# A two-layer attention and feed-forward kernel: exponentials of two chunks added before their sums are taken, and a written order for part of layer 0

## The chip, the cores and the metric

The kernel runs on one core of a Trainium2 chip. A core has five engines with a queue each: TensorE (PE in the profile, with its weight loads as PEld), VectorE (DVE), ScalarE (ACT), GpSimd (POOL) and SyncE (SP), which issues most of the transfers from memory. Each engine works through its queue in order; work of different engines runs side by side unless one waits for another. The metric is the device time of one execution in microseconds (us), the median over runs; smaller is better.

## What is computed

Eight batches of 112 tokens of 512 channels pass through two layers. Layer 0 is attention with one head over 375 memory rows per batch, then a feed-forward network (1408 hidden channels) with activations rounded to 8 bits and weights rounded to -1, 0 or 1. Layer 1 is attention with 16 heads of 32 channels over the same 375 rows, then a feed-forward network with integer weights. Cut to the part whose arithmetic changes:

```python
q, k, v = proj(hs, Wq, bq), proj(at, Wk, bk), proj(at, Wv, bv)   # 16 heads of 32
scores = clip(einsum('bhsd,bhtd->bhst', q, k) / sqrt(32), -50, 50)
scores = clip(where(attend, scores, -10000), -50, 50)
probs = softmax(scores, axis=-1)                 # over the 375 memory rows
ctx = einsum('bhst,bhtd->bhsd', probs, v)
...
x = x + layer0_attention(layernorm(x)); x = x + layer0_ffn(layernorm(x))
x = x + layer1_attention(layernorm(x)); x = x + layer1_ffn(layernorm(x))
```

The kernel takes no maximum in layer 1: it exponentiates the clipped scores, sums them over the keys (the denominator), multiplies them with the values (the numerator) and divides at the end.

## The kernel before, in words

**Layer 1 attention** (stage from 258 us to 417 us of the profile). A batch's 375 keys are three chunks of 125. The loop runs over batches b and chunks c; a step is written (b, c) here. In each step `scores(b, c)` makes, for four groups r of heads, a matmul of keys with queries into PSUM (L734), a clip on DVE (L739) into an SBUF tile `e` of 125 x 448, and an exponential in place on ACT (L740). `fill(1)` then puts one step of the key and value projection for later batches on PE (L176 for keys, evicted by ACT in L178; L183 for values, L185). `sums` of the step before puts on PE eight matmuls of `ones` with the four `e` (L754, the denominator `den`) and 32 of values with `e` (L759, the numerator `num`). `den` and `num` are evicted by ACT (L765, L766) after a batch's third chunk, and `divide` takes a reciprocal (L770) and a product (L772) on DVE one step later. `STEPS` says in which steps of a batch a `fill` is made: three per batch, but two in batches 4, 5 and 6. The tiles `e` have eight buffers, two steps' worth.

Around this run, two and three batches later, the output projection and its normalisation. `project_begin(i)` in step (i+2, 2) is a matmul L648 on PE, then on DVE L651, statistics, L659, and on GpSimd a reciprocal square root of seven short instructions (L97, L100, L101), L657, and a 128 x 512 addition L658. `project_end(i)` in step (i+3, 0) is on DVE L664, which needs L658, more statistics, and another such chain on GpSimd. `write4` is L678, `transpose4` is L685 on PE, L688 on ACT and L689 on DVE.

Integer weights of the last network are brought in meanwhile. `load_integers` issues a transfer of a piece of 128 x 512 integers on SP into one of three buffers `raw`; `convert_integers` makes a square on ACT (L721, with a read of its sum) and a conversion on GpSimd (L723), after which the buffer is free. `due` says how many pieces are converted in which step. In a step the order of the queues is: conversion, scores, fill, sums, then the rest. In (7, 2) a check `over` on GpSimd (L792) reads the sums of all squares, and a matmul of it (L795) stands on PE ahead of L648.

All five engines follow the written order in this stage.

**Layer 0** (up to 258 us). The attention loop over b makes `scores0(b)` (L365, a maximum L371 on DVE, an exponential L375 on ACT), `readout0(b-1)` (L394, L396 on DVE, and a transfer of the finished rows to `tokens` issued by GpSimd, L402), `transpose0(b+1)` of the normalised tokens written by `write0(b+1)` (L141 on DVE, then L358 on PE, L360 on ACT), a `fill` and `turn0(b)` (L387, L389). Between these, a string `BETWEEN` (three entries per batch) puts steps of two other works: a digit m is one step of rounding weight matrix m (`ternary`: four sums of magnitudes on ACT, L230; one step of a totals matmul L234 with L236, L237 and L240 on DVE; four steps of L244 on DVE and L245 on ACT), and a p is one step of `prepare(0, 2)`, which readies two tiles of 128 tokens for the feed-forward network in four steps: moments and reciprocal root on DVE; normalised values on DVE with squares (L263) on ACT and maxima (L264) on DVE; scales, a chain of short DVE instructions; rounding, L305 on ACT and L307 on DVE.

Layer 0's network runs over seven tiles i. `gate_up0(i)` makes six matmul groups on PE (L501), three activations on ACT (L505) and three products on DVE (L506), then a square (L263) on ACT, a maximum (L264) and a chain of short instructions that ends in the scale `fwd` (L274) on DVE, then the rounding L512 on ACT and L515 on GpSimd. `fill`, `turn_gate0` and `turn_down0` (L317, L319) and `down0` (L526) follow. All groups of L501, L176, L183, L394 and L526 share four PSUM tiles called `mm`: a group waits until the engine that empties a tile has done so. PE and SP follow the written order everywhere; DVE, ACT and GpSimd follow it in the attention loop of layer 0 and in layer 1's attention, and are ordered by a planner elsewhere, which may also put work written later among written work.

The functions below are `prepare`, `ternary`, the loop of layer 0, `gate_up0`, `load_integers`, `scores` and `sums`.

Of the kernel before, what the change touches and what calls it, by code (L numbers as in the profile page):

```python
# [35 lines left out]
P = 128  # L36
# [20 lines left out]
CLIP = 50.0 / SC1  # L57
WIDE = 4000.0 ** 2
# [4 lines left out]
def two_layers(ctx: ExitStack, tc: tile.TileContext, x, ctxT, ctxN, mask0, mask1, w1, w2, w3,  # L63
# [147 lines left out]
    with tc.tile_pool(name="w0", bufs=1, side="right") as w0p, \  # L211
# [9 lines left out]
        def ternary(m):  # L221

            rows = stat.tile([P, KC], F32, name="w_rows")
# [15 lines left out]
            scale = stat.tile([P, 1], F32, name="w_scale")  # L239
# [16 lines left out]
        def quantizers(srcs, n, name, squares):  # L256
# [3 lines left out]
            ss = stat.tile([P, m], F32, name=f"{name}_ss")  # L260
            mx = stat.tile([P, m], F32, name=f"{name}_mx")
# [7 lines left out]
            lim = stat.tile([P, m], F32, name=f"{name}_lim")  # L269
            nc.vector.tensor_mul(lim, mx, r)  # L270
            nc.vector.tensor_scalar_max(lim, lim, Q_EPS)
            fwd = stat.tile([P, m], F32, name=f"{name}_fwd")
# [3 lines left out]
            def back(mean, which):  # L276
                t = stat.tile([P, m], F32, name=f"{name}_back{which}")
                nc.vector.tensor_scalar(t, lim, mean, 1.0 / 127.0, ALU.mult, ALU.mult)
                return t
            yield fwd, back  # L280

        rooms = {}

# [26 lines left out]

        def transposed_h(q, n, name, pool):
# [14 lines left out]
        with tc.tile_pool(name="work0", bufs=2, side="right") as work0:  # L326
# [7 lines left out]
            def load_x(b0, b1):  # L334
                t = work0.tile([T, b1 - b0, D], F32, name=f"x0_{b0}", bufs=1)
                nc.sync.dma_start(out=t, in_=x[b0:b1].rearrange("b t d -> t b d"))
                x0.extend(t[:, b, :] for b in range(b1 - b0))
# [24 lines left out]
            def scores0(b):  # L362
# [7 lines left out]
                top = stat.tile([T, 1], F32, name="top")  # L370
# [3 lines left out]
                den = stat.tile([T, 1], F32, name="den")  # L374
# [59 lines left out]
            for i in range(4):  # L434
# [12 lines left out]
            BETWEEN = ["", "", "000", "0", "0", "1", "1", "0", "0", "0", "0", "1", "1", "1", "1",  # L447
                       "1", "1", "1p", "p", "2", "2p", "p", "2", "2"]
            preparing = prepare(0, 2)

            def between(b, n):
                for m in BETWEEN[3 * b + n]:
                    if m == "p":
                        next(preparing)
                    else:
                        steps_of(int(m), 1)

            with tc.manual_schedule(engines={ENGINES.PE, ENGINES.SP, ENGINES.DVE,
                                             ENGINES.Activation, ENGINES.Pool}):
                between(0, 2)  # L460
                for b in range(1, B):
                    if b < B - 1:
                        write0(b + 1)
                    scores0(b)
                    between(b, 0)
                    shares0(b)
                    if b > 1:
                        readout0(b - 1)
                    if b + 1 < B:
                        load_ctxN(b + 1)  # L470
                    if b + 2 < B:
                        cTs[b + 2] = load_ctxT(b + 2)
                    elif b + 2 == B:
                        cTs[2] = load_ctxT(2)
                    if b == 2 or b == 4:
                        load_raw(2, b // 2 - 1)
                    if b < B - 1:
                        transpose0(b + 1)
                    between(b, 1)
                    fill(1)  # L480
                    turn0(b)
                    between(b, 2)
                fill(1)
                turn_gate0(0)

                nc.scalar.activation(stat.tile([T, 1], F32, name="top"), s0[B - 1][1], AF.Silu)
                readout0(B - 1)


        with tc.tile_pool(name="work1", bufs=2, side="right") as work1:  # L490
            q3 = {}

            def gate_up0(i):
                qT = q1[i]
                gu = work1.tile([P, H], F32, name="gu")
                for n0, n in HBLK:
                    gate = ps_mm.tile([P, 512], F32, name="mm")
                    up = ps_mm.tile([P, 512], F32, name="mm")
                    for ps, w in ((gate, wqs[0]), (up, wqs[1])):
                        for kc in range(KC):  # L500
# [6 lines left out]
                                                   act[:, :n], ALU.mult, ALU.mult)  # L507
                q = work1.tile([P, H], BF16, name="q3")
                ranges = quantizers([gu], H, "q3", [q])
                next(ranges)  # L510
                fwd, back = next(ranges)
# [18 lines left out]
            for i in range(NT):  # L530
                if i == 2:
                    list(prepare(4, NT))
                gate_up0(i)
                if i == 0:
                    steps_of(2, 1)
                fill(1)
                if i == 0:
                    turn_gate0(1)
                    list(prepare(2, 4))
                fill(1)  # L540
                if i == 0:
                    steps_of(2, 1)
                elif i == 1:
                    steps_of(2, 2)
                if i:
                    turn_down0(i - 1)
                if 0 < i < NT - 1:
                    turn_gate0(i + 1)
                if i:
                    fill(1)  # L550

                if i == 1:
                    steps_of(2, 1)
                elif i == 2:
                    down0(0)
                if i > 1:
                    down0(i - 1)
# [71 lines left out]
    sd_s = load(tailp, sd.to_broadcast([P, D]), [P, D], "sd", nc.gpsimd)  # L629
# [7 lines left out]
    pieces = list(range(35))  # L637
# [54 lines left out]
    with tc.tile_pool(name="work2", bufs=1, side="right") as work2, \  # L692
# [6 lines left out]
        todo = [(w, which, half, c, min(D, HALVES[which][half + 1] - c))  # L699
                for which, w in enumerate((wg, wu, wd)) for half in range(2)  # L700
                for c in range(HALVES[which][half], HALVES[which][half + 1], D)]
        due = {(0, 1): 2, (0, 2): 2, (1, 0): 2, (1, 1): 2, (1, 2): 2, (2, 0): 2,
               (3, 1): 2, (3, 2): 2, (4, 0): 2, (5, 1): 2, (5, 2): 2, (6, 0): 2,
               (6, 1): 2, (6, 2): 2, (7, 0): 2, (7, 1): 2, (7, 2): 3}
# [296 lines left out]
```

## Time and profile before

| what | value |
|---|---|
| median of three runs | 538.13 us (537.45 to 540.0) |
| profiled execution, whole | 537.93 us |
| its span, first to last instruction | 536.1 us |
| mean granted TensorE clock | 0.995 |
| L754, denominator matmuls | 192, 23.8 us busy together |
| L658, addition on GpSimd, 128 x 512 | 7, median 1.279 us |
| L770, reciprocal on DVE | 8, 2.944 us each |
| L739 on DVE, four of a step | 2.45 us |
| L740 on ACT, four of a step | 2.35 us |
| L721 on ACT, and the read of its sum | 0.722 us and 0.190 us |
| L723 on GpSimd | median 0.617 us |
| `raw`, issue to landing | 2.5 to 25.2 us, median 2.9 |

A group's row names the line, the engine and the operation, what it writes and reads, how often, its busy time and the mean of one. Matmuls overlap: eight L754 take 0.96 us from the first start to the last end, and move the chain of waits by 0.89 us. A step's time on PE is best taken from that chain.

### The profile page before, as it was taken

The page shows a single profiled execution, that of the slowest core. Times are in us where ns is not written, and L with a number is a line of the kernel's source. Part 1 is how long each engine was busy: PE and PEld are TensorE (multiplying, and loading weights), DVE is VectorE, ACT ScalarE, POOL GpSimd, SP SyncE. Part 2 cuts the span into 40 slices and gives each one's busy share as a digit, 9 for nine tenths or more (in the row PEclk, how much of TensorE's full clock was granted, in tenths as well). Part 3 has the DMA queues.
Part 4 walks back from the last instruction along what each step waited for, and adds up shares of the span by engine and source line. Part 5 has one row for each costly group of instructions (what it writes and reads, how often), then busy time and mean ns, then how long its engine had stood idle before and what let it go on. Part 6 is the DMA issues. An engine that isn't in the chain of part 4 may idle for free.

```text
span 536.1 us, 8884 instructions
## 1 busy us (share of the span) xinstructions
PE 516.8 (96%) x3430; PEld 315.0 (59%) x3430; DVE 312.1 (58%) x769; ACT 247.2 (46%) x439; POOL 91.4 (17%) x197
## 2 busy tenths in 40 slices
PE   8998998989999999999999999999999999999995
PEld 6544554544455554545565555565654688889984
DVE  2552458769834755544546657988985764434432
ACT  1234754759644444402576545556766233203320
POOL 0000210101111101140121033523653540000000
PEclk9998999999999999999999999999999999999999
DMA  8994976300010120240123202102221000010001
GB/s 246 333 404 172 354 257 244 97 17 0 15 44 1 60 117 1 78 159 0 40 71 90 79 2 70 40 2 70 80 78 42 1 2 0 1 59 21 0 21 44
DMA packets 13312, 45.76 MB, mean 85 GB/s; under 512 B 1985, under 2 KB 2512, under 8 KB 12112
## 3 DMA queue, kind: packets, MB, share of 16 engines
q1 hardware_dynamic: 11744, 41.17, 22.5%
q0 software_dynamic: 1360, 3.96, 2.2%
q8 instruction: 29, 0.48, 0.4%
q14 instruction: 19, 0.16, 0.1%
q10 hardware_dynamic: 160, 0.01, 0.0%
HBM read 41.46 MB, written 1.84 MB: 81 GB/s over the span
## 4 chain that ended last, share of the span: by engine, by line
PE 82%; DVE 9%; issue 2%; ACT 2%; DMA 2%; POOL 2%; ACTq 0%; DVEq 0%; POOLq 0%
PE mm L183 14%; PE s L849 13%; PE mm L176 13%; PE down L867 7%; PE mm L648 5%; PE mm L600 5%; PE mm L501 4%; PE s L734 4%; PE mm L526 3%; PE s L365 3%; PE den L754 3%; PE mm L394 3%; PE num L759 2%; DMA tokens<-x 2%; DVE e L739 1%
## 5 line engine op out<-in xcount | busy, mean ns | idle before, releaser
L176 PE MATMUL mm<-cT,wk 128*128 128x375 f32 x256 | 88.8, 493 | 0.8 <-ACT act L505 0.8
L183 PE MATMUL mm<-wv,cT 128*125 128x512 f32 x192 | 86.8, 598 | 0.0
L740 ACT ACTIVATE e<-e 125x448 f32<-125x448 f32 x96 | 54.0, 574 | 45.3 <-DVE e L739 44.1
L849 PE MATMUL s<-h4T,w 128*128 128x512 f32 (+1 forms) x352 | 72.5, 367 | 1.2 <-DVE ln_f L95 1.2
L739 DVE TENSOR_SCALAR e<-s,upper 125x448 f32<-125x448 f32 x96 | 58.9, 677 | 18.8 <-PE s L734 18.8
L849 PEld LDWEIGHTS s<-h4T,w 128*128 128x128 f32 x352 | 63.5, 188 | 9.7 <-issue 1.8
L176 PEld LDWEIGHTS mm<-cT,wk 128*128 128x128 f32 x256 | 47.2, 192 | 29.2 <-issue 1.3
L183 PEld LDWEIGHTS mm<-wv,cT 128*125 128x125 f32 x192 | 34.8, 187 | 39.1 <-issue 37.5
L867 PE MATMUL down<-w,gu 128*128 128x512 f32 x154 | 37.0, 397 | 0.0
L501 PE MATMUL mm<-w_q,q_qT 128*128 128x512 fp8e4 (+1 forms) x168 | 34.6, 361 | 1.5 <-ACT act L505 1.5
L867 PEld LDWEIGHTS down<-w,gu 128*128 128x128 f32 x154 | 28.7, 188 | 6.6
L723 POOL TENSOR_SCALAR w<-raw 128x512 fp32r<-128x512 int32 (+1 forms) x35 | 22.3, 647 | 58.3 <-ACT w L721 57.9
L857 ACT CAST gu<-gu 128x512 fp32r<-128x512 f32 (+1 forms) x22 | 12.5, 568 | 40.5 <-DVE gu L855 40.5
L721 ACT ACTIVATE w<-raw,zero_point 128x512 fp32r<-128x512 int32 (+1 forms) x35 | 24.2, 694 | 10.6 <-DMA raw<-in_wd_dram 7.2
L734 PE MATMUL s<-qT,kv 32*125 32x112 f32 x768 | 28.5, 279 | 0.2
L501 PEld LDWEIGHTS <-q_qT 128*128 128x128 bf16 x168 | 16.4, 98 | 20.1 <-issue 2.8
L855 DVE SCALAR_TENSOR_TENSOR gu<-s,su,gu 128x512 f32<-128x512 f32 (+1 forms) x22 | 15.1, 684 | 22.2 <-PE s L849 20.2
L515 POOL TENSOR_SCALAR q<-gu 128x704 bf16<-128x704 f32 x14 | 10.9, 798 | 97.7 <-ACT gu L512 97.7
L734 PEld LDWEIGHTS s<-qT,kv 32*125 32x125 f32 x768 | 23.9, 183 | 6.2 <-issue 4.6
L759 PEld LDWEIGHTS num<-e,kv 125*32 125x32 f32 x768 | 20.5, 110 | 11.5 <-issue 11.0
L648 PE MATMUL mm<-wo,qT 128*128 128x512 f32 x56 | 25.8, 603 | 0.9 <-DVE qT L772 0.8
L402 POOL DMA_DIRECT2D tokens<-x x14 | 9.2, 657 | 100.0 <-DVE x L396 62.4
(210 smaller groups left out, 738.8 us busy)
## 6 DMA issues: line engine op xcount, KB each, us to landing
cT<-in_ctxT_dram SPq DMA_DIRECT2D x14, 750.0 KB, 5.6
raw<-in_w_dram SPq DMA_DIRECT2D x6, 1408.0 KB, 18.1
cN<-in_ctxN_dram SPq DMA_DIRECT2D x8, 768.0 KB, 4.7
raw<-in_wd_dram SPq DMA_DIRECT2D x11, 256.0 KB, 2.7
raw<-in_wg_dram SPq DMA_DIRECT2D x10, 256.0 KB, 2.9
raw<-in_wu_dram SPq DMA_DIRECT2D x10, 256.0 KB, 2.9
out_dram<-d SPq DMA_DIRECT2D x7, 256.0 KB, 2.0
wk<-in_wk_dram SPq DMA_DIRECT2D x2, 512.0 KB, 8.2
```

The costliest lines, as they stand in the source:

```text
L176: nc.tensor.matmul(ps, lhsT=wk_s[:, kc, dc * P:(dc + 1) * P], rhs=cT[:, kc, :], start=(kc == 0), stop=(kc == KC - 1))
L183: nc.tensor.matmul(ps, lhsT=cT[:, kc, c * CK:(c + 1) * CK], rhs=wv_s[:, kc, :], start=(kc == 0), stop=(kc == KC - 1))
L501: nc.tensor.matmul(ps[:, :n], lhsT=qT[:, kc, :], rhs=w[:, kc * H + n0:kc * H + n0 + n], start=(kc == 0), stop=(kc == KC - 1))
L600: nc.tensor.matmul(ps, lhsT=wq_s[:, kc, dc * P:(dc + 1) * P], rhs=h2T[g][:, kc, :], start=(kc == 0), stop=(kc == KC - 1))
L648: nc.tensor.matmul(ps, lhsT=qT[:, kc, i * P:(i + 1) * P], rhs=wo_s[:, kc, :], start=(kc == 0), stop=(kc == KC - 1))
L721: nc.scalar.activation(t, raw, AF.Square, bias=zero_point, accum_out=squares[:, k:k + 1])
L734: nc.tensor.matmul(ss[r][:, dc, :], lhsT=kT[rows, dc, c * CK:(c + 1) * CK], rhs=qT[rows, dc, b * T:(b + 1) * T], start=True, stop=True)
L739: nc.vector.tensor_scalar(e, ss[r], upper[:, c, b:b + 1], -CLIP, ALU.min, ALU.max)
L740: nc.scalar.activation(e, e, AF.Exp, scale=SC1)
L759: nc.tensor.matmul(num[r * HD:(r + 1) * HD, dc, :], lhsT=v[:, c, head], rhs=es[r][:, dc, :], start=(c == 0 and dc == 0), stop=(c == NCK - ...
L849: nc.tensor.matmul(ps[:, :n], lhsT=w[:, c:c + P], rhs=h4T[k][:, kc, :n], start=(kc == 0 and k == 0), stop=(kc == KC - 1 and k == 1))
L867: nc.tensor.matmul(ps, lhsT=gus[k][:, hc, j * P:(j + 1) * P], rhs=w[:, c:c + D], start=(hc == 0 and k == 0), stop=(hc == HC - 1 and k == 1))
```

## The change

In layer 1's attention the tiles `e` become three fixed sets of four that rotate: step (b, c) writes set (b + c) mod 3. After the scores of a batch's third chunk, `add(b)` adds the second chunk's four exponentials to the first's in place, on GpSimd for batches 4, 5 and 6 and on DVE for the others. `sums` makes the denominator only after the third chunk, from the added set and the third chunk's set. The reciprocal's tile is the first tile of the added set. Integer pieces are 640 wide in two buffers, 29 of them in place of 35. The row of scales `sd` is loaded by SP at the start of the last network instead of by GpSimd earlier.

In layer 0, tokens are normalised one batch earlier, the totals of the first weight matrix move behind `turn0(1)`, the third block of x and many small tiles move to another pool (`w0p`, open until layer 0 ends), and `gate_up0` is split in three (`gate_up0`, `ranges0`, `round0`). The written order of all five engines is kept up to the end of tile 1 of the network.

```diff
-            BETWEEN = ["", "", "000", "0", "0", "1", "1", "0", "0", "0", "0", "1", "1", "1", "1",
-                       "1", "1", "1p", "p", "2", "2p", "p", "2", "2"]
-            preparing = prepare(0, 2)
+            BETWEEN = ["", "", "000", "0", "1", "01", "1", "0", "0", "0", "0", "1", "1", "1", "1",
+                       "1", "1p", "", "p", "2", "2p", "p", "2P", "2"]
...
+        preparing = [prepare(0, 2), prepare(2, 4), prepare(4, NT)]
...
+                pool = w0p if b1 == B else work0
+                t = pool.tile([T, b1 - b0, D], F32, name=f"x0_{b0}", bufs=1)
...
+            written.enter_context(tc.manual_schedule(engines={
+                ENGINES.PE, ENGINES.SP, ENGINES.DVE, ENGINES.Activation, ENGINES.Pool}))
+            write0(2)
+            between(0, 2)
+            for b in range(1, B):
+                scores0(b)
+                between(b, 0)
+                shares0(b)
+                if b > 1:
+                    readout0(b - 1)
+                if b + 2 < B:
+                    write0(b + 2)
...
+            next(preparing[1])
+            readout0(B - 1)
...
+            gate_up0(0)
+            next(preparing[1])
+            ranges0(0)
+            steps_of(2, 1)
+            fill(1)
+            turn_gate0(1)
+            next(preparing[1])
+            steps_of(2, 1)
+            round0(0)
+            fill(1)
+            steps_of(2, 1)
+            gate_up0(1)
+            ranges0(1)
+            steps_of(2, 1)
+            fill(1)
+            round0(1)
+            fill(1)
+            turn_down0(0)
+            turn_gate0(2)
+            steps_of(2, 1)
+            fill(1)
+            next(preparing[2])
+            written.close()
...
-        due = {(0, 1): 2, (0, 2): 2, (1, 0): 2, (1, 1): 2, (1, 2): 2, (2, 0): 2,
-               (3, 1): 2, (3, 2): 2, (4, 0): 2, (5, 1): 2, (5, 2): 2, (6, 0): 2,
-               (6, 1): 2, (6, 2): 2, (7, 0): 2, (7, 1): 2, (7, 2): 3}
+        due = {(0, 1): 2, (0, 2): 2, (1, 0): 1, (1, 1): 2, (1, 2): 2, (2, 0): 1,
+               (3, 1): 2, (3, 2): 2, (4, 0): 1, (5, 1): 2, (5, 2): 2, (6, 0): 1,
+               (6, 1): 2, (6, 2): 2, (7, 0): 1, (7, 1): 2, (7, 2): 2}
...
-                raw = work2.tile([P, D], I32, name="raw", bufs=3)[:, :n]
+                raw = work2.tile([P, PIECE], I32, name="raw", bufs=2)[:, :n]
...
+        sets = [[work2.tile([P, KC, T], F32, name=f"e{i}{r}") for r in range(NR)]
+                for i in range(NCK)]
+
+        def add(b):
+            add = (nc.gpsimd if b in ADD_POOL else nc.vector).tensor_add
+            for r in range(NR):
+                e, e1 = (sets[(b + c) % NCK][r][:CK] for c in range(2))
+                add(e, e, e1)
...
-            for r in range(NR):
-                nc.tensor.matmul(den[r * HD:(r + 1) * HD], lhsT=ones[:CK, :HD],
-                                 rhs=es[r], start=(c == 0), stop=(c == NCK - 1))
+            if c == NCK - 1:
+                den = ps_av.tile([P, KC, T], F32, name="den")
+                added = sets[b % NCK]
+                for k, of in enumerate((added, es)):
+                    for r in range(NR):
+                        nc.tensor.matmul(den[r * HD:(r + 1) * HD], lhsT=ones[:CK, :HD],
+                                         rhs=of[r][:CK], start=(k == 0), stop=(k == 1))
...
-                rden = work2.tile([P, KC, T], F32, name="rden")
+                rden = added[0]
...
+        ADD_POOL = (4, 5, 6)
...
                 es = scores(b, c)
+                if c == 2:
+                    add(b)
```

Here the P in `BETWEEN` is a step of `prepare(2, 4)`; its second step stands before `readout0(7)`, its third after `gate_up0(0)`, its fourth after `turn_gate0(1)`. The digit at (1, 1) that was the totals of the first matrix is now the first sum of the second, and the totals stand at (1, 2).

## The prediction

> **What bounds it now.** I read, in this order: the page's totals, PE's waits, busy time by windows, the chain of waits in layer 1's attention, DVE's waits there, and the timelines of DVE, ACT and GpSimd where these point.
>
> ```profile
> PE 516.8 (96%) x3430; PEld 315.0 (59%) x3430; DVE 312.1 (58%) x769; ACT 247.2 (46%) x439; POOL 91.4 (17%) x197
> ...
> PE s L234 <- ACT w_q L230: 2.3, 1, 2.3
> PE s L358 <- DVE h L141: 1.5, 1, 1.5
> PE mm L501 <- ACT act L505: 1.5, 1, 1.5
> ...
> PE mm L648 <- DVE qT L772: 0.8, 1, 0.8
> ...
> 40.00:42.00 2.00, 0.37 (x3) 0.37 (x4) 0.32 (x2) 2.00 (x5) 0.00 (x0) 1.00 0.97 407
> 42.00:44.00 2.00, 2.00 (x6) 1.19 (x6) 0.92 (x4) 0.00 (x0) 0.00 (x0) 0.73 0.99 408
> 44.00:46.00 2.00, 2.00 (x4) 1.00 (x3) 0.00 (x0) 0.00 (x0) 0.00 (x0) 0.50 0.73 301
> ```
>
> TensorE is the bound on average; waits are "us, times, longest", windows give busy us of PE, PEld, DVE, ACT, GpSimd, then the granted clock. Layer 0 has three waits to gain, and after the longest the clock falls to a half.
>
> ```profile
> 360.00:370.00 10.00, 9.19 (x143) 5.57 (x137) 9.45 (x15) 7.24 (x17) 4.65 (x12) 1.00 0.22 68
> 380.00:390.00 10.00, 9.88 (x125) 5.80 (x124) 9.72 (x17) 6.57 (x16) 5.16 (x12) 1.00 0.42 128
> ...
> DVE tokens L664 <- POOL tokens L658: 4.9, 5, 1.4
> ...
> 372.28 0.69 DVE L651 TENSOR_TENSOR d<-mm,bo 128x512 f32<-128x512 f32 x1 [0.96 <-PE mm L648]
> ...
> 379.03 1.09 DVE L664 SCALAR_TENSOR_TENSOR tokens<-d,ln_f,tokens 128x512 f32<-128x512 f32 x1 [0.86 <-POOL tokens L658]
> ...
> 420.44 1.32 DVE L772 TENSOR_TENSOR qT<-qT,rden 128x448 f32<-128x448 f32 x1
> ```
>
> In batches 5 and 6 DVE is as full as PE, and the chain of waits runs through it: from L651 (353.53) over GpSimd's chain to L658, L664, the clips of the next step, L770, L772, PE's L648, to the next L651 (372.28): 18.75 us, then 19.09 us. PE waits in it, and DVE waits for L658 each time: whatever makes GpSimd later there lengthens the loop one to one.
>
> **Layer 1, PE.** One group of denominators is 0.89 us in the chain; 24 groups become 16, the cut always in step (b, 2). In batches 0 to 3 PE is full. DVE gets four additions, bounded by 4 x 0.62 us (L772, same shape) and 4 x 1.32 us (the same under a GpSimd addition, the last row above); GpSimd is nearly idle there, so 2.7. In batches 0 and 1 DVE stood idle 3 to 4 us before the clips of a chunk (3.06 at 269.14, 3.97 at 292.75), which covers them; in batch 2 the clips of (2, 2) and the additions end 2 us before L651 needs DVE; in batch 3 (clips end at 329.8, additions 332.5, L678 333.0, L651 at 334.03 - 0.89 = 333.14) just in time. Gain 4 x 0.89 = **-3.6 us**.
>
> **Batches 4 to 6.** PE's gain is not on the loop. An addition on GpSimd is nearest to L658, 1.279 us for 512 columns, so about 1.2 for 448 (ends: 0.62, DVE's time, and 2.4, twice, if the two engines keep blocking each other); four are 4.8 us. Batch 4: GpSimd is free from 345.9 to 355.5, but the additions lie over L772 of 348.72 (0.62 to 1.32): L648 starts 0.25 later instead of 0.45 to 0.89 sooner: +0.25.
> Batch 5, counted from L651 at 353.53. GpSimd ends the root chain at 11.5 and converts the two pieces of (5, 1), 0.77 each at 640 columns, to 13.0. Before, one piece of (5, 2) already lay in a third buffer; now both need those two, and a transfer took 2.8 us from such a release to ACT's start (365.6 to 368.39), say 3.0 with a quarter more bytes: from 12.25 and 13.0 they land at 15.2 and 16.0. Squares (0.9 and a read of 0.19) end at 16.05 and 17.1, conversions at 16.8 and 17.9, the additions at 22.6. Behind them on GpSimd stands L97 of `project_begin(3)`, ready at 20.7. It is late by **1.9 us**, and so are L658, L664 and the loop. Batch 6 repeats it, and its 1.9 falls into batch 7. There PE has three fills and a spare again, but the last conversions move by the same 1.9: counted from L651 at 391.37, `over` ends at 20.5 instead of 18.65. Its matmul L795 stands on PE ahead of L648 and had 0.63 to spare, so L648 is late by 1.25, and behind it the last denominator now has two groups (+0.89): **+2.1**. The additions of batch 7 on DVE end at 22.2, before those groups at 24.3. Layer 1: -3.6 + 0.25 + 1.9 + 2.1 = **+0.7 us**.
>
> **A rule against it.** The Trainium skill, GPSIMD Engine Reference, section Key points, says GpSimd shares its SBUF interfaces with VectorE, in contention with its instructions of two SBUF inputs. The row agrees in kind: L772 went from 0.62 to 1.32 beside L658. By the row a clash costs 0.7 once (batch 4's); by the rule every addition may block L772, L659 and be blocked, up to the 2.4 each above. I take the row, as the clips (from PSUM) that fill most of DVE's time are one input.
>
> **Layer 0, attention.** (a) The totals L234 leave their place before the fill: PE's wait of 2.35 (39.28 to 41.63) goes. The matmuls behind took 4.35 instead of 2.71 us, another 1.64. The rule (TensorE: Matmul & The Clock Gate, section Why this matters for your kernels) is no idle gaps over about 3 us; the row shows a half clock after 2.35, though not after 1.54 and 1.52. By the rule the gain is 2.35, by the row **-4.0**; I take the row. Next late: the copy of the next tokens (L360 at 42.1), 0.3 before PE needs it. (b) `write0(7)` was at 89.67 on DVE behind two chains of short instructions; a batch earlier it is done by 80.2: **-1.54**. (c) L505 at 113.59 waited 3.72 us for the transfer of tokens, which read x where `act` was to lie. With x elsewhere it starts at about 109.1, after two squares; PE needs the tile it empties at 111.4: **-1.52**.
>
> **Layer 0, the network.** The written order is now binding on ACT and DVE. I count on the old time axis with (b) and (c) taken off; (a) is apart. PE starts `gate_up0(0)` at 109.18 - 1.54 = 107.6 and ends it 4.75 us of matmuls later (as the chain shows for tile 2), at 112.35; DVE ends its last product at 113.0. DVE then has, in this order: scales of tiles 2 and 3 (19 instructions at 0.195 apart, as at 28.45 to 30.7: 3.5 us) to 116.5; maximum 1.62 and scale chain of tile 0 (161.81 to 166.0 elsewhere: 4.2) to 120.7; three for the totals (0.6); two roundings L307 (0.8); L244 (0.95) to 123.1. ACT, in order, waits for that L244: L245 1.45 to 124.5, L512 1.56 to 126.05, and only then L178, which empties the second fill's tile, at 126.6. PE, after two fills and three groups of `gate_up0(1)`, asks for a fourth tile at 120.5: of the four, this one is the first to be free. PE waits **6.1 us**; before, the planner had L178 at 122.3, ahead of L512, and PE waited 0.77 later. After two more short waits (L245 0.7 us longer than one group, then one product) PE ends the tile at 130.1, and the next fill starts there instead of at 126.87: +3.2 with (b) and (c) already in. ACT's queue (square, scale chain, L245, L178, L512, three copies) gives tile 2's tokens at 141.6, 1.2 after PE is there: +4.2. The moments of tiles 4 to 6 (4.9 us on DVE, no longer where the planner likes) hold the first product of tile 2: 0 to 1.2, taken 0.8. The half clock after so long a wait: 0 to 1.7, taken 1.2. Layer 0: -4.0 + 4.2 + 0.8 + 1.2 = **+2.2 us**.
>
> At no cost: six fewer pieces (ACT saves about 1 us; it is 46% busy), `sd` on SP (idle there; needed after 467 us), pools changed. If (5, 2)'s landing were not hidden the cost is counted above.
>
> **Sum.** 537.93 + 2.2 + 0.7 = 540.8 for the profiled execution (1.83 beyond its span); the median lies 0.2 higher: **541.0 us**. A measurement here can tell about 0.5%, 2.7 us, from no change.
>
> **Rivals.** (1) Not slower: ACT's queue does not hold PE in tile 1. Then layer 0 keeps (a), (b), (c) and the old 0.77: -7.8; total -7.1, **531.0**. For: each wait is in the table; the point that decides is L178 of the second fill before 120.5. Against: 3.5 us of ACT work stands between L244 and it. Chance 0.27. (2) GpSimd's additions end before L97 (landing or additions 1.9 faster): layer 1 gives -3.3, total -1.1, **537.0**; chance 0.10. Both: -11.1, **527.0**; 0.06. (3) Slower: the shared interface makes an addition 2.4 us. Four are 9.6, so L97 is 4.8 later still in the loops of batches 5 and 6 (there is no spare beyond 2.8 us from 17.9) and 0.5 in batch 4: +10.1, **551**; 0.12. For: 1.32 and the 1.09 of L664. Against: most of DVE's work there reads PSUM. (4) My case, **541.0**, 538 to 545: 0.45.
> That the change misses its aim is excluded for PE's work: the groups are gone by construction.
>
> Range: 529.0 to 547.0 leaves out both gains together (0.06) and most of (3), less than 2 in 10. Faster: (1), both, and edges, 0.35; same: parts of (4) and (2), 0.22; slower: 0.43.
>
> **What would show it.** L754 with 128 matmuls; no wait of L234, L358 or of L501 at 114; one wait of L501 on ACT of about 6 us in tile 1 with a low clock behind it; additions near 1.2 us on GpSimd; waits of L664 on L658 near 2.8 us in batches 6 and 7. The prediction is wrong if PE passes tile 1 without that wait, or if the loops of batches 5 and 6 keep their 18.8 and 19.1 us.

## The result, and the profile after

The changed kernel takes 538.12 us (median of 20 runs, 537.3 to 539.25), the kernel before beside it 537.98 us (20 runs, 536.73 to 540.0): a ratio of 1.0006, 95% interval 0.9999 to 1.0014. It is neither faster nor slower; I had forecast 541.0. The profiled execution has a span of 536.3 us where it had 536.1. Yet both layers look different inside. Lines after the change have other numbers: L501 is now L508 (gate and up products), L505 is L512 (their activation; before, L512 was the rounding), L506 is L513, L178 is L179, L244 is L245 (DVE), L245 is L246 (ACT), L512 is L526 (rounding), L319 is L323; in layer 1 L97 is L98, L648 is L670, L651 is L673, L658 is L680, L659 is L681, L664 is L686, L678 is L700, L754 is L789, L772 is L807, L792 and L795 are L830 and L833, L849 (first gate product of the last network) is L889; the additions are L760.

The page's totals, and from the views of waits (us, times, longest) the rows that answer to those of before:

```profile
PE 512.5 (96%) x3366; PEld 313.4 (58%) x3366; DVE 329.2 (61%) x789; ACT 244.1 (46%) x427; POOL 105.0 (20%) x202
...
PE mm L508 <- ACT kv L179: 5.5, 1, 5.5
PE mm L670 <- DVE qT L807: 3.8, 3, 1.6
PE s L833 <- POOL over L830: 1.5, 1, 1.5
...
DVE tokens L686 <- POOL tokens L680: 7.7, 5, 2.2
```

PE is busy 4.3 us less, and all of it has become waiting: the three waits of layer 0 (2.3, 1.5, 1.5) are gone, one of 5.5 is new, and in layer 1 PE waits 3.8 us for L807 (0.8 before) and 1.5 us for `over`. DVE waits 7.7 us for L680 where it waited 4.9.

The same windows as before (busy us of PE, PEld, DVE, ACT, GpSimd, then the granted clock):

```profile
40.00:42.00 2.00, 2.00 (x7) 1.15 (x7) 0.77 (x3) 2.00 (x5) 0.00 (x0) 1.00 0.97 405
42.00:44.00 2.00, 2.00 (x11) 1.41 (x10) 0.48 (x3) 2.00 (x4) 0.00 (x0) 1.00 1.03 420
44.00:46.00 2.00, 2.00 (x6) 0.76 (x6) 0.41 (x1) 1.90 (x4) 0.00 (x0) 1.00 0.50 201
360.00:370.00 10.00, 8.44 (x131) 5.25 (x133) 8.98 (x12) 6.81 (x14) 6.22 (x11) 1.00 0.35 101
380.00:390.00 10.00, 8.32 (x103) 5.04 (x96) 9.01 (x12) 6.51 (x15) 5.08 (x11) 1.00 0.35 94
```

From 40 to 46 us PE is full and its clock is 1.00 where it had been 0.73 and 0.50. In layer 1's late batches PE has dropped from 9.2 and 9.9 to 8.4 and 8.3 of 10 us: the denominators that went made room for waits there, not for a shorter loop.

**Layer 0.** PE starts the network's first product at 103.44 (before 109.18) and ends it without a wait. Then comes tile 1. PE's timeline before, for tiles 0, 1 and 2:

```profile
109.18 3.62 PE L501 MATMUL mm<-w_q,q_qT 128*128 128x512 fp8e4 x16
...
121.18 4.92 PE L501 MATMUL mm<-w_q,q_qT 128*128 128x512 fp8e4 x24
...
137.25 4.92 PE L501 MATMUL mm<-w_q,q_qT 128*128 128x512 fp8e4 x24
```

And after, for tiles 1 and 2, with ACT's below it:

```profile
113.76 2.75 PE L508 MATMUL mm<-w_q,q_qT 128*128 128x512 fp8e4 x12
121.97 4.29 PE L508 MATMUL mm<-w_q,q_qT 128*128 128x512 fp8e4 x12 [5.46 <-ACT kv L179]
...
137.36 1.90 PE L508 MATMUL mm<-w_q,q_qT 128*128 128x512 fp8e4 x8 [0.81 <-ACT q_qT L323]
```

```profile
118.54 1.47 ACT L246 ACTIVATE w_q<-raw,unrounder 128x1408 fp8e4<-128x1408 f32 x1 [4.87 <-DVE raw L245]
119.92 1.55 ACT L526 ACTIVATE gu<-gu,rounder,q_fwd 128x1408 f32<-128x1408 f32 x1
121.37 0.55 ACT L179 ACTIVATE kv<-mm,bk 128x375 f32<-128x375 f32 x1
```

ACT stands idle for 4.87 us at the head of its queue, waiting for DVE; L179, for which nothing is missing, is third in that queue, and PE waits for it. Tile 2 starts at 137.36; before it started at 137.25. So 7.4 us won by 108 us are spent by 137, and the first scores of layer 1 come at 258.99 (before 258.67).

The moments of tiles 4 to 6 are in tile 2 as forecast, but hold nothing. Tile 2's first product on DVE (the first row) waits for PE, and the moments (L129) lie between its products:

```profile
139.41 0.75 DVE L513 SCALAR_TENSOR_TENSOR gu<-mm,q_back,act 128x512 f32<-128x512 f32 x1 [0.72 <-PE mm L508]
...
140.16 0.66 DVE L129 BATCH_NORM_STATS2 bn<-tokens 128x6 f32<-128x512 f32 x1
...
141.16 0.75 DVE L513 SCALAR_TENSOR_TENSOR gu<-mm,q_back,act 128x512 f32<-128x512 f32 x1
```

**Layer 1.** The table gives the stage from the first scores to the first gate product (us), cut at the L673 of (3, 2), (4, 2), (5, 2) and (6, 2); the runs of the experiments are in it for later. Each row is one profiled execution.

| kernel | to (3, 2) | batch 4 | batch 5 | batch 6 | rest | sum |
|---|---|---|---|---|---|---|
| before | 75.4 | 19.50 | 18.75 | 19.09 | 25.9 | 158.6 |
| after | 71.6 | 19.74 | 18.76 | 20.29 | 28.1 | 158.5 |
| pieces alone, no additions | 75.4 | 19.50 | 18.75 | 19.18 | 25.6 | 158.4 |
| no additions in 4 to 7 | 71.6 | 20.28 | 18.77 | 18.90 | 25.9 | 155.5 |
| all additions on DVE | 71.6 | 20.17 | 20.46 | 20.58 | 25.9 | 158.7 |
| two of four on DVE in 4 to 6 | 71.6 | 19.13 | 20.31 | 21.49 | 27.4 | 160.0 |

What took the 3.8 us back in this execution, in GpSimd's timeline (first two rows) and DVE's:

```profile
368.01 5.03 POOL L760 TENSOR_TENSOR e<-e,e 125x448 f32<-125x448 f32 x4
373.02 0.18 POOL L98 TENSOR_SCALAR ln_h<-ln_var 128x1 f32<-128x1 f32 x1
...
377.26 0.88 DVE L686 SCALAR_TENSOR_TENSOR tokens<-d,ln_f,tokens 128x512 f32<-128x512 f32 x1 [2.23 <-POOL tokens L680]
391.57 1.64 DVE L681 SCALAR_TENSOR_TENSOR d<-d,ln_mv,gamma 128x512 f32<-128x512 f32 x1
...
345.07 1.47 DVE L807 TENSOR_TENSOR qT<-qT,e 128x448 f32<-128x448 f32 x1
```

L98 had its input at 370.98 and starts at 373.02, right behind four additions; L686 then waits 2.23 us instead of 0.86. The other two rows are clashes of the two engines: L681 took 0.74 in the same place before, L807 takes 0.62 undisturbed.

The place of the loss is not the same in every execution. Six runs below have the same layer 1, and in three of their profiled executions the low clock has a part in it. With layer 1 alone and with spare matmuls in layer 0, batch 5 took 20.81 and 20.48 us and batch 6 only 18.88 and 18.90; the stage took 158.6 and 159.1. PE's L670 of (5, 2) ran at a low clock in them (0.56 from 366 to 368 us in the first, 0.50 in the second) and took 5.40 us. In the third (only the second fill moved) it was L670 of (6, 2), with 6.12 us, and the stage took 158.9. PE's row after, and in the run with spare matmuls (L675 is L670 there):

```profile
365.36 3.70 PE L670 MATMUL mm<-wo,qT 128*128 128x512 f32 x8 [1.56 <-DVE qT L807]
...
364.57 5.40 PE L675 MATMUL mm<-wo,qT 128*128 128x512 f32 x8 [1.57 <-DVE qT L812]
```

With the loop late for that reason, L98 no longer came late in (5, 2). So the queue of GpSimd is what took batch 6's 1.2 us in the changed kernel's own execution, and a low clock behind the new waits of PE can take its place; what decides between them is not shown.

### The profile page after: what moved, and what is told of

Its sections match the earlier page's. It is cut to its first block, busy times and chain, and to the rows that moved or that the text cites. A ratio compares the mean times of both kernels' runs of the same rounds, so it can differ in the third digit from the quotient of the medians.

```text
span 536.3 us, 8697 instructions
## 1 busy us (share of the span) xinstructions
PE 512.5 (96%) x3366; PEld 313.4 (58%) x3366; DVE 329.2 (61%) x789; ACT 244.1 (46%) x427; POOL 105.0 (20%) x202
## 4 chain that ended last, share of the span: by engine, by line
PE 76%; DVE 8%; POOL 7%; ACT 3%; issue 2%; DMA 2%; POOLq 0%; DVEq 0%
PE s L889 13%; PE mm L177 11%; PE mm L184 11%; PE down L907 7%; PE mm L508 6%; PE mm L623 5%; PE mm L400 4%; PE s L371 4%; PE mm L670 3%; PE mm L540 3%; PE s L768 2%; POOL ln_t L101 2%; POOL e L760 2%; PE num L794 2%; DMA raw<-in_wd_dram 1%
## 5 line engine op out<-in xcount | busy, mean ns | idle before, releaser
L177 PE MATMUL mm<-cT,wk 128*128 128x375 f32 x256 | 87.0, 485 | 0.0
L889 PE MATMUL s<-h4T,w 128*128 128x512 f32 (+1 forms) x352 | 72.6, 367 | 0.6 <-ACT qT L801 0.6
L889 PEld LDWEIGHTS s<-h4T,w 128*128 128x128 f32 x352 | 63.5, 188 | 9.2 <-PE num L794 0.9
L774 ACT ACTIVATE e<-e 125x448 f32<-125x448 f32 x96 | 52.1, 571 | 30.1 <-DVE e L773 29.5
L508 PE MATMUL mm<-w_q,q_qT 128*128 128x512 fp8e4 (+1 forms) x168 | 36.5, 374 | 6.3 <-ACT kv L179 5.5
L508 PEld LDWEIGHTS <-q_qT 128*128 128x128 bf16 x168 | 16.8, 100 | 26.6 <-issue 9.0
L745 POOL TENSOR_SCALAR w<-raw 128x640 fp32r<-128x640 int32 (+2 forms) x29 | 20.2, 699 | 60.5 <-ACT w L743 59.9
L768 PE MATMUL s<-qT,kv 32*125 32x112 f32 x768 | 30.3, 280 | 0.6
L743 ACT ACTIVATE w<-raw,zero_point 128x640 fp32r<-128x640 int32 (+2 forms) x29 | 22.6, 781 | 18.2 <-DMA raw<-in_wd_dram 12.1
L408 POOL DMA_DIRECT2D tokens<-x x14 | 11.8, 844 | 91.6 <-DVE x L402 63.1
L670 PE MATMUL mm<-wo,qT 128*128 128x512 f32 x56 | 25.8, 603 | 3.8 <-DVE qT L807 3.8
L768 PEld LDWEIGHTS s<-qT,kv 32*125 32x125 f32 x768 | 25.0, 183 | 7.2 <-issue 4.4
L623 PE MATMUL mm<-h2T,wq 128*128 128x512 f32 (+1 forms) x64 | 24.8, 544 | 1.6 <-issue 0.9
```

Source lines behind the costliest of these rows:

```text
L177: nc.tensor.matmul(ps, lhsT=wk_s[:, kc, dc * P:(dc + 1) * P], rhs=cT[:, kc, :], start=(kc == 0), stop=(kc == KC - 1))
L508: nc.tensor.matmul(ps[:, :n], lhsT=qT[:, kc, :], rhs=w[:, kc * H + n0:kc * H + n0 + n], start=(kc == 0), stop=(kc == KC - 1))
L623: nc.tensor.matmul(ps, lhsT=wq_s[:, kc, dc * P:(dc + 1) * P], rhs=h2T[g][:, kc, :], start=(kc == 0), stop=(kc == KC - 1))
L670: nc.tensor.matmul(ps, lhsT=qT[:, kc, i * P:(i + 1) * P], rhs=wo_s[:, kc, :], start=(kc == 0), stop=(kc == KC - 1))
L743: nc.scalar.activation(t, raw, AF.Square, bias=zero_point, accum_out=squares[:, k:k + 1])
L768: nc.tensor.matmul(ss[r][:, dc, :], lhsT=kT[rows, dc, c * CK:(c + 1) * CK], rhs=qT[rows, dc, b * T:(b + 1) * T], start=True, stop=True)
```

## The experiments

My theory after the traces: layer 0 and layer 1 each come out even by themselves, layer 0 by the order on ACT's queue in tiles 1 and 2, layer 1 by the additions on GpSimd in batches 4 to 6. The rivals are in the expectations. Each edit is one of the changed kernel where nothing else is said. All ratios are to the kernel before, with 95% intervals.

### Each layer alone

The change's layer 0 with the loop, tiles and pieces of layer 1 as before:

```diff
-        sets = [[work2.tile([P, KC, T], F32, name=f"e{i}{r}") for r in range(NR)]
-                for i in range(NCK)]
...
+                e = work2.tile([CK, KC, T], F32, name="e", bufs=8)
...
+                raw = work2.tile([P, D], I32, name="raw", bufs=3)[:, :n]
```

> The change's layer 0 with layer 1 as before. Mine, from the two traces: layer 0 gains 7.4 us up to the second tile of the network and loses 7.7 again by the third, so 538.3 (+0.3 against before), and layer 1's first scores 0.3 us later than in before. Rival, my prediction's own sum: layer 0 costs 2.2 us and layer 1 hides it, so 540.2.

538.24 us, ratio 0.9998 (0.9981 to 1.0016). As expected, and not the 540.2 of my prediction's sum. The first scores came at 259.8, later than expected: the query projection waited 0.7 us behind the transfer of its bias, as in several executions below (up to 0.9) but not in the changed kernel's own.

And the reverse, the written order of layer 0 as before with the change's layer 1:

```diff
-            BETWEEN = ["", "", "000", "0", "1", "01", "1", "0", "0", "0", "0", "1", "1", "1", "1",
-                       "1", "1p", "", "p", "2", "2p", "p", "2P", "2"]
+            BETWEEN = ["", "", "000", "0", "0", "1", "1", "0", "0", "0", "0", "1", "1", "1", "1",
+                       "1", "1", "1p", "p", "2", "2p", "p", "2", "2"]
...
-            gate_up0(0)
-            next(preparing[1])
-            ranges0(0)
...
+            for i in range(NT):
```

> Layer 0 ordered as before, with the change's layer 1. Mine: 3.7 us gained up to the fourth batch, 3.6 given back in batches 4 to 7, so 537.9 (-0.1 against before). Rival, that the two layers pull in opposite directions and only cancel: 535.8 if layer 0 costs what I predicted.

537.27 us, ratio 0.9985 (0.9972 to 0.9998): 0.7 us faster, nearer to mine than to the rival's 535.8. Neither layer hides a loss of the other.

### Layer 0: which instruction holds PE?

Only the second fill is moved ahead of the conversion and the rounding:

```diff
             turn_gate0(1)
             next(preparing[1])
+            fill(1)
             steps_of(2, 1)
             round0(0)
-            fill(1)
             steps_of(2, 1)
```

> After, with only the second fill written ahead of the weight's conversion and tile 0's rounding, so that its eviction no longer stands behind them on ACT. Mine: the wait moves by one PSUM tile, to the first silu of the second tile, which still stands behind the same conversion and rounding: PE waits 5 to 6 us one tile later, time unchanged (537.5 to 538.5). Rival, that the eviction that the trace names as the releaser is the cause: the wait goes, 532 to 533.

538.59 us, ratio 1.0012 (0.9995 to 1.0029): unchanged. PE's timeline shows the wait one tile on, with another releaser's name:

```profile
113.22 3.61 PE L508 MATMUL mm<-w_q,q_qT 128*128 128x512 fp8e4 x16
122.90 2.72 PE L508 MATMUL mm<-w_q,q_qT 128*128 128x384 fp8e4 x8 [6.07 <-ACT act L512]
```

The releaser that a wait names (L179) was not its cause; the cause is L246, at which the whole queue stands.

Now the second fill and both products of tile 1 go ahead of everything that waits for DVE:

```diff
             turn_gate0(1)
+            fill(1)
+            gate_up0(1)
             next(preparing[1])
             steps_of(2, 1)
             round0(0)
-            fill(1)
             steps_of(2, 1)
-            gate_up0(1)
```

> After, with the second fill and the gate and up products of the second tile written ahead of the roundings of tiles 2 and 3, of the third weight's conversion and of tile 0's rounding. Mine: ACT's queue alone made PE wait, so the wait of 5.5 us and the half clock behind it go, tile 2 starts near 130 instead of 137.4, and the time is 531 (-6 to -7.5 against after). Rival: ACT and DVE have as much to do as before and are the real limit up to tile 2, so the wait only moves to the transposes of tile 0 or to tile 2's first product; 537 to 538.

539.27 us, ratio 1.0027 (1.0016 to 1.0039). My number was wrong. PE passed tile 1 without a wait, as meant, and then stood before tile 2. PE's timeline, and ACT's:

```profile
113.44 4.92 PE L508 MATMUL mm<-w_q,q_qT 128*128 128x512 fp8e4 x24
...
135.56 7.68 PE L508 MATMUL mm<-w_q,q_qT 128*128 128x512 fp8e4 x24 [5.66 <-ACT q_qT L323]
```

```profile
130.36 1.47 ACT L246 ACTIVATE w_q<-raw,unrounder 128x1408 fp8e4<-128x1408 f32 x1 [3.64 <-DVE raw L245]
131.74 0.55 ACT L179 ACTIVATE kv<-mm,bk 128x375 f32<-128x375 f32 x1
132.19 1.55 ACT L526 ACTIVATE gu<-gu,rounder,q_fwd 128x1408 f32<-128x1408 f32 x1
133.64 1.86 ACT L323 COPY q_qT<-s 128x768 bf16<-128x768 bf16 x3
```

It is the same picture: L323's copies were ready to be made from about 126.4 on, and stood behind an L246 that waited for DVE. Tile 2 starts only 1.8 us sooner, and at a low clock takes 7.68 us instead of 4.9. Whether this is still the order (mine) or too much work for ACT and DVE (the rival) was then open, and the next run decides it: the copies and tile 2's products also go ahead (the diff is against the run before; the loop over later tiles leaves `gate_up0(2)` out).

```diff
             round0(0)
             steps_of(2, 1)
             ranges0(1)
-            steps_of(2, 1)
             fill(1)
-            round0(1)
             fill(1)
             turn_down0(0)
             turn_gate0(2)
-            steps_of(2, 1)
             fill(1)
+            gate_up0(2)
+            steps_of(2, 1)
+            round0(1)
+            steps_of(2, 1)
             next(preparing[2])
```

> The mended order, and in addition the first transposes of tile 0 and tile 2's copy (three copies on ACT) and tile 2's gate and up products written ahead of the scale chain of tile 1's conversions and rounding. Mine: in the run before PE waited 5.66 us for L323 only because that copy stood behind the same kind of queue on ACT (L246 waiting for DVE's L245, then L526); with it moved, tile 2 starts at about 130 instead of 137.4, no wait over 1 us is left up to tile 3, and the time is 531 (-6.5 to -7.5 against after). Rival: ACT and DVE together are the limit up to tile 3; the wait moves on again to tile 1's transposes (POOL's rounding), and the time is 536 to 539.

531.17 us, ratio 0.9875 (0.9852 to 0.9897): 7 us faster than after, at the expected value. PE's timeline:

```profile
113.67 4.92 PE L508 MATMUL mm<-w_q,q_qT 128*128 128x512 fp8e4 x24
...
129.97 4.92 PE L508 MATMUL mm<-w_q,q_qT 128*128 128x512 fp8e4 x24
```

No operation was added or removed, only the written order is another (PE's, DVE's and GpSimd's with it). So the work of ACT and DVE fits, and the order was the cause; that it was ACT's queue is what the waits show.

### Layer 0: what the low clock costs

My prediction had added 1.4 us of short waits behind the long one and 1.2 us for a half clock. One run moves ACT's L246 of 121.8 away, to see which of the two paces the tile:

```diff
             round0(0)
             fill(1)
-            steps_of(2, 1)
             gate_up0(1)
+            steps_of(2, 1)
             ranges0(1)
```

> After, with the third conversion step (ACT's L246 of 121.8 and its partner) written behind the gate and up products of tile 1, so that tile 1's first silu comes 1.4 us sooner after the long wait. Mine: the second half of the tile is paced by the half clock (12 matmuls in 4.3 us instead of 2.2), not by ACT, so my prediction counted the same microseconds twice (1.4 of short waits and 1.2 of half clock): time unchanged, 538.1, and the 12 matmuls again take 4.2 to 4.4 us. Rival: ACT paces them, and the clock's share is hidden: they take 2.9 us, and the time is 536.7.

541.89 us, ratio 1.0068 (1.0046 to 1.0091). The twelve matmuls took 4.13 us (4.29 in after), so the clock does pace them; but the time was not unchanged, as I had expected, since the step that moved delays everything behind it on DVE and ACT:

```profile
121.90 4.13 PE L508 MATMUL mm<-w_q,q_qT 128*128 128x512 fp8e4 x12 [5.47 <-ACT kv L179]
...
139.32 6.57 PE L508 MATMUL mm<-w_q,q_qT 128*128 128x512 fp8e4 x24 [3.00 <-ACT q_qT L323]
```

Tile 1's square (L264) starts at 129.03 instead of 127.02, behind the moved L246, which waits 1.99 us for DVE. Tile 2 came 2.0 us later and, after a wait of 3.00 us, ran 6.57 us instead of 4.93: 3.6 of the 4.7 us by which this profiled execution (542.82) is longer.

The other run keeps PE busy in the wait:

```diff
                     for ps, w in ((gate, wqs[0]), (up, wqs[1])):
+                        if (i, n0) == (1, 512) and ps is up:
+                            idle = ps_s.tile([P, 512], F32, name="s")
+                            for _ in range(24):
+                                nc.tensor.matmul(idle, lhsT=qT[:, 0, :], rhs=w[:, :512],
+                                                 start=True, stop=True)
```

> After, with 24 spare matmuls on PE (their sums are read by nothing) put where PE waits 5.46 us in tile 1, to keep the clock up; everything else as it is. Mine: the clock stays at 1.00, the twelve matmuls behind take 2.2 to 3.6 us instead of 4.3, the next fill starts 0.7 to 2 us sooner, but tile 2 still starts at 137.4, because ACT's queue (its L323) sets that: time unchanged, 538.1. Rival, my prediction's term: the half clock is on the path, and without it the time is 536.1 to 536.9.

538.19 us, ratio 1.0009 (0.9995 to 1.0022). PE's timeline and one window (L513 is the product here):

```profile
122.04 1.02 PE L513 MATMUL mm<-w_q,q_qT 128*128 128x512 fp8e4 x4 [0.29 <-ACT kv L179]
123.97 1.46 PE L513 MATMUL mm<-w_q,q_qT 128*128 128x384 fp8e4 x8 [0.91 <-ACT act L517]
...
136.52 4.93 PE L513 MATMUL mm<-w_q,q_qT 128*128 128x512 fp8e4 x24 [0.81 <-ACT q_qT L323]
...
122.00:124.00 2.00, 1.05 (x5) 0.41 (x5) 0.05 (x1) 2.00 (x3) 1.15 (x2) 1.00 0.00 0
```

The clock stays at 1.00 and the short waits appear, as expected. But tile 2 starts 0.84 us sooner than in after, not at 137.4: half of my expectation failed. So the low clock does cost 0.84 us on the path, and the short waits behind it 1.1 (3.2 us from the first of the twelve to the next fill, against 2.2 at full clock without waits): 1.9 together, where the prediction had added 1.4 and 1.2. The two overlap: in the run before, ACT's step was out of the way, and the stretch was only 0.16 us shorter. The time of the whole cannot tell 0.84 us: the first scores came 0.8 us sooner, but layer 1 took 159.1 us in this profiled execution, with the low clock shown above.

### Layer 1: additions, engines and pieces

No additions in batches 4 to 7, three groups of denominators there as before:

```diff
+            if b in PLAIN or c == NCK - 1:
+                groups = (es,) if b in PLAIN else (added, es)
...
-        ADD_POOL = (4, 5, 6)
+        ADD_POOL, PLAIN = (), (4, 5, 6, 7)
...
-                if c == 2:
+                if c == 2 and b not in PLAIN:
                     add(b)
```

> After, with three groups of denominators and no additions in batches 4 to 7, as before; additions on DVE only in batches 0 to 3. Mine: the 3.7 us gained by the fourth batch stay, the loops of batches 5 and 6 return to 18.75 and 19.1 us and L686's waits to 0.9, so 534.4 (-3.7). Rival, that the last batch is tied to the two buffers of the integer weights (each transfer starts only when GpSimd has released one): the gain is then lost by the end of batch 7 in any case, 537.5 to 538.

535.08 us, ratio 0.9957 (0.9945 to 0.997). DVE's timeline gives the loops (starts of L673 in (4, 2), (5, 2) and (6, 2)):

```profile
350.16 0.69 DVE L673 TENSOR_TENSOR d<-mm,bo 128x512 f32<-128x512 f32 x1 [2.13 <-PE mm L670]
...
368.93 0.69 DVE L673 TENSOR_TENSOR d<-mm,bo 128x512 f32<-128x512 f32 x1 [0.70 <-PE mm L670]
...
387.83 0.69 DVE L673 TENSOR_TENSOR d<-mm,bo 128x512 f32<-128x512 f32 x1 [0.59 <-PE mm L670]
```

The loops of batches 5 and 6 are 18.77 and 18.90 again and the rest 25.9: the gain of the first batches stays, 3.2 us of it. That 0.5 is missing against 3.7 lies in batch 4: its loop now holds the two late groups of batch 3 besides its own two, one more than before (0.89).

No additions at all, only the wider pieces in two buffers (the rest of the edit is that of the run before):

```diff
-        ADD_POOL = (4, 5, 6)
+        ADD_POOL, PLAIN = (), (0, 1, 2, 3, 4, 5, 6, 7)
```

> After, with three groups of denominators and no addition in any batch: of layer 1's part only the pieces of 640 columns in two buffers (and the fixed sets of tiles) stay. Mine: the transfers remain hidden behind the other work of each batch, so layer 1 takes as long as before (158.6 us from the first scores to the first gate product) and the time is that of the change's layer 0 alone, 538.2. Rival: the two buffers cost 0.4 or more in the last batch, where the run without additions in batches 4 to 7 took 23.55 us instead of 23.18: 159 us or more, 538.6.

538.29 us, ratio 1.0005 (0.9994 to 1.0017), and 158.4 us for the stage: the pieces by themselves cost nothing.

All additions on DVE:

```diff
-        ADD_POOL = (4, 5, 6)
+        ADD_POOL = ()
```

> After, with the additions of batches 4 to 6 on DVE instead of GpSimd. Mine: DVE is full in these batches, each loop gets 2.2 to 2.7 us longer than before the change, and the delays through GpSimd go: 538.1 + 3 x 2.5 - 2.7 = 542.9. Rival, that the two engines' contention for SBUF is the main price of the additions on GpSimd: then DVE's own 2.2 us cost less than what they cause there, 537 or below.

538.46 us, ratio 1.0009 (1.0 to 1.0018): neither theory's number. Four additions take DVE 2.2 to 2.6 us, but DVE had been waiting 0.8 us for L670 in each loop, so batches 5 and 6 grow by 1.7 and 1.5 only, and the last stretch, free of GpSimd's delay, is as short as before. I had charged the additions without the wait that they fill.

Two of the four on each engine:

```diff
             for r in range(NR):
+                add = (nc.gpsimd if b in ADD_POOL and r < 2 else nc.vector).tensor_add
```

> After, with only the first two of the four additions of batches 4 to 6 on GpSimd and the other two on DVE. Mine: GpSimd ends its two about 2.4 us sooner, before L98 is ready, and DVE's two (1.1 us) lie mostly in its wait for L670: the loop of batch 6 returns from 20.3 to about 19.1 to 19.4, L686's long waits go, the last batch loses its 1.3 of lateness: 535.7 to 536.3. Rival, that the two engines side by side are the price (each slows the other), not the order on GpSimd's queue: no gain, 538.

538.86 us, ratio 1.0014 (0.9999 to 1.003), the stage 160.0 us: my expectation failed, the rival's number held. The queue was indeed mended (L686 waits 0.88 us at most), but the two pairs of additions run at the same time. DVE's row and GpSimd's in batch 6, and a window behind the pair of batch 5:

```profile
387.47 2.79 DVE L760 TENSOR_TENSOR e<-e,e 125x448 f32<-125x448 f32 x2
...
387.18 2.61 POOL L760 TENSOR_TENSOR e<-e,e 125x448 f32<-125x448 f32 x2
...
370.00:374.00 4.00, 4.00 (x37) 2.67 (x37) 3.86 (x10) 2.37 (x6) 2.34 (x7) 0.57 0.00 0
```

An addition on DVE takes 1.4 us there instead of 0.55; on GpSimd it takes 1.3, hardly more than alone. So only DVE is slowed, not each by the other. The low clock of 0.57 adds to it: eight matmuls of a fill took 4.08 us instead of 2.79. With the queue mended and no gain, the obvious way round it is closed by DVE's slower additions and the low clock together; their shares are not separated.

### Both mended

The second order of layer 0 and no additions in batches 4 to 7:

> The twice mended order of layer 0 together with layer 1 without additions in batches 4 to 7. Mine: the two gains add up, 531.2 - 3.0 = 528.1, ratio 0.982. Rival, that a shared limit (the last batch's loads of the integer weights, which start no sooner) takes a part: 530 or more.

529.46 us, ratio 0.9838 (0.9819 to 0.9857): faster than both kernels, by 8.6 us against the one before. The two ratios multiply to 0.9832, inside this interval: the gains add up, and the rival's shared limit is not seen beyond the interval. My number in us was 1.4 too low. In its profiled execution the stage of layer 1 takes 155.4 us, all of its gain, and the first scores come 0.8 us later than with the layer 0 order alone (252.87 against 252.08), mostly behind the bias of the queries. PE's row, and DVE's:

```profile
231.73 7.13 PE L625 MATMUL mm<-h2T,wq 128*128 128x512 f32 x16 [0.47 <-DVE qT L627]
...
230.92 1.41 DVE L627 TENSOR_SCALAR qT<-mm,bq 128x512 f32<-128x512 f32 x2 [3.00 <-DMA bq<-in_bq_dram]
```

The other 0.6 us are within the intervals of the three runs.

## Why the prediction was wrong

The forecast was a slow-down of 0.53%, and none came. The step that failed is the sizing of the delays: four terms were too large by 2.7 us together, nearly the whole of the forecast loss of 2.9. In three of them a delay came and was shorter; in the fourth, the moments, the delay did not come at all. That the gains and losses of each layer then cancel to within 0.3 us is a coincidence of sizes: nothing in the runs ties them together.

- **Attention of layer 0**, -4.0, -1.54, -1.52: right. The first product starts 5.74 us sooner (5.54 predicted), and without its wait the next work 7.42 sooner (7.06 predicted). The row of before decided better than the rule here: the clock had been low after a wait of 2.35 us, and from 40 to 46 us it is full now.
- **The wait of tile 1**, 6.1 us: measured 5.46, with ACT's order and DVE's chain as written down. Too large by 0.6.
- **Short waits (1.4, within the +3.2) and "the half clock, taken 1.2"**: they partly lie beside each other, and the prediction added them. The run with PE kept busy shows 1.1 and 0.84. Too large by 0.6.
- **"The moments of tiles 4 to 6 hold the first product of tile 2 ... taken 0.8"**: measured 0. DVE's first product of tile 2 waited for PE and not for the moments, PE ran tile 2 in 4.9 us without a wait, and the next fill starts at 142.12 (before 142.01). This is the largest single error; I had a range of 0 to 1.2 and no row that put the moments ahead of the product.
- **Tile 2's tokens, +4.2** (its own 3.2 and 1.2 make 4.4): the path through ACT's queue was right, and with the measured sizes put in it gives the measured start. Layer 0 was to cost 2.2 and cost 0.1 at tile 2 and 0.3 by the first scores.
- **Batches 0 to 3, -3.6**: right, -3.75. **Batch 4, +0.25**: 0.24. **Batch 5**: 18.76, no change in the changed kernel's execution. The sum has its 1.9 in the next loop, though the prediction's last sentence has both loops longer; only batch 6's was.
- **Batch 6, "late by 1.9"**: L98 is late by 2.04, but the loop only by 1.2. Behind the additions GpSimd's chain no longer waits 0.27 us for DVE after its first instruction, its second takes 0.34 us instead of 0.70, and from L98 to the end of L680 it takes 4.2 us instead of 4.7; L686 itself took 0.88 instead of 1.09. Its waits for L680 were 2.23 us in batches 6 and 7 (2.8 forecast). I had moved the old chain as it was. Too large by 0.7.
- **The last batch, +2.1**: 2.16, but by luck. Counted from the last L673 or L651, L670 starts 1.9 us later (1.25 predicted), and behind it the second group of denominators costs 0.2 (0.89 predicted), since PE's wait before the first gate product shrinks from 1.15 to 0.62 us.

The rival that ACT's queue does not hold PE (531.0) did not come about, but a written order in which it does not reaches its number: 531.17 us. Nor did an addition take 2.4 us (rival 3): it took 1.2 to 1.3 on GpSimd. On the shared interface (the Trainium skill, GPSIMD Engine Reference, section Key points) I took the row of a single clash, 0.7 us, over the rule. For this kernel that was enough: its clashes are L807 in batch 4 and L681 before the last batch, 0.85 and 0.9 us. The run with the additions split agrees with the rule, since there both engines do additions of two SBUF inputs at once and DVE's take 1.4 us.

As to the form of the forecast: two terms, of 0.8 and 1.2 us, had been taken from ranges that began at 0, each above the middle of its range, and added to a difference of gains and losses several times as large. Of the loss of 2.9 us, 2.0 rested on these two choices.

## What to carry to other kernels

On an engine with an order written out, the releaser that a wait names may only stand in the queue; look for the instruction of that queue that waited itself, and move every ready instruction that PE needs ahead of it, in all places where it repeats: mending one of two gave nothing here (539.27 us), mending both 7 us. Take work off TensorE only in those stages where it is full, and charge the engine that gets it with the waits that it can fill and those that it makes. When an instruction is delayed, the chain behind it should be counted without the gaps in which it used to wait for others. Two delays in one stretch should be added only where they cannot lie beside each other.

## What the runs showed of the hardware

Two-input additions of 125 x 448 on DVE took 0.55 us alone and 1.4 us beside the same on GpSimd, which lost hardly anything (1.2 to 1.3). The same 24 matmuls took 4.9 us at full clock, 6.57 after a wait of 3.00 us and 7.68 after one of 5.66. The length of one gap does not decide it: with all additions on DVE, waits of 1.28 and 1.97 us close together left the clock at 1.00, with split additions 1.29 and 1.81 us were followed by 0.57, and before the change 2.35 us by 0.50. In (5, 2) of the changed layer 1, the same wait of 1.56 or 1.57 us left the clock at 1.00 in one execution and was followed by 0.50 in another. The Trainium skill (TensorE: Matmul & The Clock Gate, section Why this matters for your kernels) asks for no idle gaps over about 3 us; in this kernel shorter ones could cost clock too.
